# One graph transformer forward pass on one core: what the first gather of each edge beat waits for

## The chip, the cores and the metric

The kernel runs on one core of one Trainium2 chip. The metric is device time in microseconds (us); lower is better. TensorE is called PE below, VectorE DVE, ScalarE ACT, GpSimd POOL and SyncE SP, as the profile calls them.

## The reference, cut to what matters

The reference is a two-layer graph transformer on 625 nodes of width 1024 with 10,000 edges. The change lies in the first graph layer, an attention over edges (GATv2). Cut to its core, with H = 4 heads of 64:

```python
xl = (h @ Wl).reshape(n, H, D)            # h: the normed nodes, projected to 256
xr = (h @ Wr).reshape(n, H, D)
msg = xl[src] + xr[dst]                   # one row per edge
e = einsum('ehd,hd->eh', where(msg > 0, msg, 0.2 * msg), att)
alpha = softmax of e over the edges of each dst
out = segment_sum(alpha[..., None] * xl[src], dst) @ W_up
```

To this the reference adds a linear attention over the same nodes (q, k and v by 1024x1024 matrices, 16 heads). A quantised feed-forward block, a second graph layer, a second linear attention, an attention and a mixture of eight experts follow.

## The kernel before, in words

**The stages.** The kernel works in fp32 on tiles of 125 nodes (five of them, named by t). The edge stage of layer 0 stretches over the linear attention of layer 0, which gives PE its work while the edges are handled by the other engines. After it come the weighted sums over the edges, the feed-forward block, layer 1, and the experts, which take the second half of the time.

**The edge stage.** `xl` and `xr` lie in DRAM as `xl_d` and `xr_d`, 625 rows of 1 KB each. The edges are cut into 79 chunks of up to 128, and the chunks into 40 groups of two (the last group, number 39, has one chunk of 16 edges). A group goes through three steps:

- `gather(g, j, side)` (line 605, its DMA on line 611): an indirect DMA from POOL's queue fetches 128 rows of `xl_d` into tile `ga` (side 0) or of `xr_d` into `gb` (side 1). Each of `ga` and `gb` has five buffers, so that gather g overwrites what group g - 5 has used.
- `score_group(g)` (line 617; lines 621 and 591 to 594): four DVE operations make the edge scores `es`. ACT then raises them (`exp`, line 598).
- `scatter` (line 626, its DMA on line 631): an indirect DMA from POOL's queue writes 128 raised scores into the DRAM array `table`, one row of four per pair of nodes.

**The beats.** `one_beat()` (line 684) issues one step of this pipeline: on DVE the score of an earlier group, on ACT its exponential, and on POOL the four gathers of group g with scatters of earlier groups between them. `lags` says how far behind they run: the scores of group g - 4, the exponentials of g - 5 and the scatters of g - 6 belong to beat g; near the end (line 807) the lags become 1, 1 and 2. All engines execute in the order in which the program issues, which is written by hand: after each group of matmuls, `work(us)` (line 702) adds up an estimate of PE's time and issues a beat for every 8.6 us of it. In steady state a beat has six POOL instructions: ga, gb, table, ga, gb, table.

**The wait in question.** `group` (line 130) and the two other places that issue matmuls in this stage note the name of the last matmul in `latest["pe"]`. The first gather of each beat (`j == 0 and side == 0`) is made to wait for that matmul by `behind(got, latest["pe"])` (line 615). Since POOL's queue is in order, what stands behind this gather waits with it: the other gathers of the beat, and the scatters.

**The order around it.** PE runs the key and value projections (`pk`, `pv`), with counts of edges between them (`pct`), the states (`pkv`), the queries (`pq`), the answers (`pd`, `po`) and the output projection (`px`, line 745). DVE takes each result out of PSUM one step later than PE makes it (the class `Stream`), and a beat's score follows those. Between the keys and the queries the PSUM pool is exchanged, so the first `pq` needs the last `pv` to be read out. At the end the beats that are left are issued in a row (line 817). Then `load_table` (line 827) reads `table` back (tile `tb`), also from POOL's queue; DVE multiplies it with the counts (`pT`, line 841), and PE sums over it (`pg`).

Of the kernel before, what the change touches and what calls it, by code (L numbers as in the profile page):

```python
# [53 lines left out]
def attempt(ctx: ExitStack, tc: tile.TileContext, w: dict, out: bass.AP, shifted: bool):  # L54
# [78 lines left out]
    latest = {}  # L133

    def behind(ins, name):

        tc.add_manual_dep(ins.ins, name, mybir.DependencyInfo(mybir.DependencyClass.Sync,
                                                              mybir.DependencyReason.DATA), reason="pace")
        return ins
# [216 lines left out]
    with ExitStack() as st0:  # L356
# [8 lines left out]
        with ExitStack() as edges:  # L365
# [239 lines left out]
            def gather(g, j, side):  # L605
                lo, n, p = groups[g]
                if j == 0 and side == 0:
                    ab[g] = [pool.tile([128, G, 256], FP, tag=k, name=k, bufs=5) for k in ("ga", "gb")]
                if j < n:
                    src, ix = ((xl_d, si), (xr_d, di))[side]  # L610
                    got = nc.gpsimd.indirect_dma_start(  # L611
                        out=ab[g][side][0:p, j, :], out_offset=None, in_=src[:, :],
                        in_offset=bass.IndirectOffsetOnAxis(ap=ix[0:p, lo + j:lo + j + 1], axis=0))
                    if j == 0 and side == 0 and "pe" in latest:
                        behind(got, latest["pe"])

            def score_group(g):
                lo, n, p = groups[g]
# [65 lines left out]
            def one_beat():  # L684
                g = beat["g"]
                beat["g"] += 1
                if 5 <= g < NT + 5:
                    self_loops(g - 5)
                if lags[1] > lags[0]:
                    raise_all(g - lags[1])  # L690
                    scores(g - lags[0])
                else:
                    scores(g - lags[0])
                    raise_all(g - lags[1])
                for j in range(G):
                    if g < len(groups):
                        gather(g, j, 0)
                        scatter(g - lags[2] - 1)
                        gather(g, j, 1)
                    scatter(g - lags[2])  # L700
# [1271 lines left out]
```

## Time and profile before

| what | value |
|---|---|
| median of 3 runs | 2227.58 us (2226.61 to 2228.72) |
| the profiled execution, its own time | 2228.76 us |
| its span in the profile | 2227.0 us |
| mean granted PE clock | 0.977 |
| PE busy | 2112.5 us, 95% of the span |
| POOL busy | 341.4 us, 15% |
| first and last gather start | 57.6 and 423.4 us |
| first and last scatter start | 94.3 and 442.0 us |
| gathers on each side, scatters | 79, 79, 79; about 1 us of POOL each |

The profile is of one execution, which took 1.2 us more than the median. Its span is 1.8 us shorter than its own time. Times inside the profile are counted from the start of the span. A line of the timeline gives start, duration, engine, line, operation, and in brackets how long the engine had been idle and what ended that. For a DMA from POOL's queue the duration is that of POOL's instruction, and not of the transfer.

### The profile page before, as it was taken

What the parts mean: (1) busy time and instruction counts of PE and PEld (TensorE: products, weight loads), DVE (VectorE), ACT (ScalarE), POOL (GpSimd) and SP (SyncE); (2) the same over time, 40 slices, a digit from 0 to 9 for tenths busy, and PEclk for the clock granted to TensorE, in tenths of its full rate; (3) what the DMA queues carried; (4) which work ended last, traced back from release to release, by engine and by line L of the source; (5) the groups of instructions that cost most, each with busy time, mean ns of one, the idle gap of its engine ahead of it and who ended that gap; (6) DMA issues with size and microseconds to landing.
All of it is one profiled execution on the core that took longest, in us unless ns stands there. A gap on an engine that the chain in (4) does not pass through costs nothing. (4 is left out here: it accounts for less than half of the span.)

```text
span 2227.0 us, 17363 instructions
## 1 busy us (share of the span) xinstructions
PE 2112.5 (95%) x6934; PEld 1209.9 (54%) x6934; DVE 713.3 (32%) x1214; ACT 194.1 (9%) x354; POOL 341.4 (15%) x349
## 2 busy tenths in 40 slices
PE   8899799578899999999999999999999999999998
PEld 6466375245444777754445767557744444444443
DVE  5765467557623560000113133322011111111112
ACT  2000010001211100000000111100000000000000
POOL 1666656610000020210000000110000000000011
PEclk9999899878999999999999999999999999999999
DMA  9226252071122110231213111021099987997742
GB/s 299 77 62 209 59 182 81 25 212 33 38 85 71 52 38 1 85 142 38 76 38 104 38 38 38 20 103 61 34 347 337 331 325 282 327 331 286 275 144 92
DMA packets 145848, 301.62 MB, mean 135 GB/s; under 512 B 12370, under 2 KB 22436, under 8 KB 145754
## 3 DMA queue, kind: packets, MB, share of 16 engines
q1 hardware_dynamic: 123700, 244.23, 30.7%
q0 software_dynamic: 17376, 46.42, 7.1%
q10 hardware_dynamic: 4678, 9.72, 1.4%
q8 instruction: 58, 0.95, 0.2%
q14 instruction: 36, 0.29, 0.0%
HBM read 277.49 MB, written 22.84 MB: 135 GB/s over the span
## 5 line engine op out<-in xcount | busy, mean ns | idle before, releaser
L130 PE MATMUL pu<-w,xgT 128*128 128x512 f32 x768 | 333.9, 593 | 1.9 <-DVE xgT L1266 1.9
L130 PEld LDWEIGHTS pu<-w,xgT 128*128 128x128 f32 x768 | 144.0, 190 | 174.8 <-issue 171.7
L130 PE MATMUL pyb<-w,hb 128*128 128x512 f32 x384 | 174.3, 599 | 2.5 <-ACT yb L105 2.1
L130 PE MATMUL pq<-xnT,w 128*128 128x313 f32 x512 | 139.6, 432 | 13.8 <-DVE v L286 13.0
L130 PE MATMUL pk<-w,xnT 128*125 128x512 f32 x320 | 143.2, 599 | 3.3 <-issue 2.8
L130 PE MATMUL pv<-w,xnT 128*125 128x512 f32 x320 | 142.2, 597 | 1.5 <-issue 1.1
L130 PE MATMUL p<-tT,w 128*128 128x313 f32 x512 | 136.3, 428 | 0.4 <-DVE tT L1266 0.4
L130 PEld LDWEIGHTS pq<-xnT,w 128*128 128x128 f32 x512 | 98.2, 193 | 53.5 <-DVE v L286 13.8
L130 PEld LDWEIGHTS pyb<-w,hb 128*128 128x128 f32 x384 | 69.8, 189 | 90.9 <-issue 74.8
L1806 DVE TENSOR_TENSOR su<-pu,su 128x512 f32<-128x512 f32 x24 | 16.6, 692 | 314.6 <-ACT su L1805 314.6
L130 PEld LDWEIGHTS p<-tT,w 128*128 128x128 f32 x512 | 96.8, 190 | 37.9 <-issue 1.2
L130 PEld LDWEIGHTS pk<-w,xnT 128*125 128x125 f32 x320 | 59.8, 189 | 77.0 <-issue 76.1
L130 PEld LDWEIGHTS pv<-w,xnT 128*125 128x125 f32 x320 | 59.9, 189 | 75.4 <-issue 72.6
L1789 POOL DMA_INDIRECT xg<-rows_d,slots x12 | 11.4, 946 | 524.8 <-PE pxg L1796 449.0
L631 POOL DMA_INDIRECT table<-es,at x79 | 84.2, 1066 | 49.4 <-issue 26.2
L611 POOL DMA_INDIRECT ga<-xl_d,si x79 | 79.7, 1009 | 74.8 <-issue 33.2
L611 POOL DMA_INDIRECT gb<-xr_d,di x79 | 81.8, 1036 | 25.3 <-issue 22.8
L745 PE MATMUL px<-w,oT 128*125 128x512 f32 x160 | 69.8, 594 | 2.9 <-DVE x L909 2.0
L130 PE MATMUL px<-w,hT 128*125 128x512 f32 x160 | 70.3, 592 | 0.0
L130 PE MATMUL px<-w,oT 128*125 128x512 f32 x160 | 70.3, 592 | 0.0
L130 PE MATMUL ph<-meanT,w 128*128 128x313 f32 x256 | 70.1, 426 | 0.0
L130 PE MATMUL ph<-xnT,w 128*128 128x313 f32 x256 | 70.0, 427 | 0.0
(366 smaller groups left out, 2459.9 us busy)
## 6 DMA issues: line engine op xcount, KB each, us to landing
w<-in_eW_dram SPq DMA_DIRECT2D x144, 1024.0 KB
w<-in_L_Wk_dram SPq DMA_DIRECT2D x8, 1024.0 KB
w<-in_L_Wv_dram SPq DMA_DIRECT2D x8, 1024.0 KB
w<-in_L_Wq_dram SPq DMA_DIRECT2D x8, 1024.0 KB
w<-in_L_Wo_dram SPq DMA_DIRECT2D x8, 1024.0 KB
w<-in_W_self_dram SPq DMA_DIRECT2D x8, 1024.0 KB
w<-in_W_neigh_dram SPq DMA_DIRECT2D x8, 1024.0 KB
w<-in_sW_dram SPq DMA_DIRECT2D x8, 1024.0 KB
```

Source lines behind the costliest of these rows:

```text
L130: made = nc.tensor.matmul(dst, lhsT=lhsT, rhs=rhs, start=(i == 0), stop=(i == len(pairs) - 1))
L611: got = nc.gpsimd.indirect_dma_start(out=ab[g][side][0:p, j, :], out_offset=None, in_=src[:, :], in_offset=bass.IndirectOffsetOnAxis(ap=ix ...
L631: nc.gpsimd.indirect_dma_start(out=table[:, :], out_offset=bass.IndirectOffsetOnAxis(ap=at[0:p, lo + j:lo + j + 1], axis=0), in_=es[0:p, l ...
L745: made = nc.tensor.matmul(hold["px", t][:P, c, :], lhsT=oT[:, k, nodes(t)], rhs=wo[c](k), start=(k == 0), stop=(k == KC - 1 and keep is no ...
L1789: nc.gpsimd.indirect_dma_start(out=xg, out_offset=None, in_=rows_d[:, :], in_offset=bass.IndirectOffsetOnAxis(ap=slots[:, b:b + 1], axis=0))
L1806: nc.vector.tensor_tensor(su, pu[:, 0, :], su, op=ALU.mult)
```

## The change

The first gather of a beat no longer waits for the matmul noted last. It waits instead for the DMA of the gather issued last before it, which is the last `gb` of the beat ahead; waiting for a DMA means waiting until its data have landed. The first beat waits for neither. Nothing is moved: every engine issues the same instructions in the same order, and no other wait is taken away by hand. The buffers and the order of the writes to `table` still give waits of their own, as before.

```diff
                     got = nc.gpsimd.indirect_dma_start(
                         out=ab[g][side][0:p, j, :], out_offset=None, in_=src[:, :],
                         in_offset=bass.IndirectOffsetOnAxis(ap=ix[0:p, lo + j:lo + j + 1], axis=0))
-                    if j == 0 and side == 0 and "pe" in latest:
-                        behind(got, latest["pe"])
+                    if j == 0 and side == 0 and g:
+                        behind(got, latest["gather"])
+                    latest["gather"] = got.ins.name
```

Later lines of the changed kernel have numbers that are higher by one.

## The prediction

> **What bounds the kernel now.** I read the page first, for the stage.
>
> ```profile
> span 2227.0 us, 17363 instructions
> ...
> PE 2112.5 (95%) x6934; PEld 1209.9 (54%) x6934; DVE 713.3 (32%) x1214; ACT 194.1 (9%) x354; POOL 341.4 (15%) x349
> ...
> PE   8899799578899999999999999999999999999998
> ...
> POOL 1666656610000020210000000110000000000011
> PEclk9999899878999999999999999999999999999999
> ```
>
> PE is busy nearly everywhere; it dips only in the first ten slices of 55.7 us, and that is where POOL works. Whatever the change does, it does before about 460 us. Afterwards everything is relative to PE, so what is won or lost there reaches the end whole. Next, the table of windows over that stage (columns: window, its length, busy us of PE, PEld, DVE, ACT, POOL, granted clock, DMA share, GB/s).
>
> ```profile
> 260.00:280.00 20.00, 7.67 (x23) 5.40 (x24) 2.84 (x5) 0.00 (x0) 12.95 (x13) 0.66 0.20 59
> ...
> 420.00:440.00 20.00, 2.57 (x6) 0.77 (x5) 15.00 (x20) 0.41 (x2) 11.74 (x9) 0.64 0.02 3
> 440.00:460.00 20.00, 4.70 (x18) 3.95 (x18) 4.84 (x5) 0.00 (x0) 8.30 (x14) 0.50 0.71 162
> ```
>
> PE stands in two places. The second is the end of the edge stage; the timelines of POOL and of all engines give its chain.
>
> ```profile
> 375.38 0.99 POOL L631 DMA_INDIRECT table<-es,at  x1 [0.44 <-DMA table<-es,at]
> 384.86 0.96 POOL L611 DMA_INDIRECT ga<-xl_d,si  x1 [8.50 <-PE px L745]
> ...
> 396.72 1.48 POOL L611 DMA_INDIRECT ga<-xl_d,si  x1 [0.30 <-issue]
> 398.51 1.34 POOL L631 DMA_INDIRECT table<-es,at  x1 [0.30 <-issue]
> ```
>
> ```profile
> 442.03 0.85 POOL L631 DMA_INDIRECT table<-es,at  x1 [1.90 <-issue]
> 444.54 0.90 POOL L173 DMA_DIRECT2D tb<-table  x1 [1.66 <-issue]
> ...
> 453.14 4.84 DVE L841 TENSOR_TENSOR pT<-tb,CT 125x500 f32<-125x500 f32 x5 [16.54 <-DMA tb<-table]
> ...
> 454.23 0.68 PE L130 MATMUL pg<-xl,pT 125*125 125x65 f32 x2 [31.66 <-DVE pT L841]
> ```
>
> PE's last px ends at 422.6; it then waits 31.7 us for a chain that runs through POOL: last scatter, table read back, pT. From 384.86 on POOL has hardly a gap, and just before it stood 8.5 us for a matmul. That is the wait that the change removes.
>
> The first place is odd:
>
> ```profile
> 252.29 7.03 PE L130 MATMUL pv<-w,xnT 128*125 128x512 f32 x16
> 272.33 10.21 PE L130 MATMUL pq<-xnT,w 128*128 128x313 f32 x32 [13.01 <-DVE v L286]
> ```
>
> ```profile
> 271.59 0.69 DVE L286 TENSOR_TENSOR v<-pv,bv_t 125x512 f32<-125x512 f32 x1 [12.73 <-remote]
> ```
>
> The pv matmuls end at 259.3, but DVE, which needs only their semaphore, starts at 271.59, and POOL's next beat, which waits for PE too, at 271.82. PE's signal came 12 us late. It comes late elsewhere: kb at 80.67 for a pk ended at 73.8, kb at 157.77 for 153.2, v at 227.01 for 215.9. Each time the signal fell due late in a run of 21 to 40 us in which POOL had issued without a gap over 0.5 us (57.6 to 78.6, 131.7 to 155.4, 196.9 to 224.3, 228.8 to 268.6), and the signal came 2 to 3 us after POOL stopped. I take it, as an inference from four coincidences, that long unbroken runs of indirect DMAs delay PE's signals. The wait on PE then acts as a valve: late signals stop POOL.
>
> **What the Trainium skill says.** "Perfetto Trace Analysis", section "DMA Instruction — SWDGE (GPSIMD)": the shown end of such a DMA is that of making descriptors, and not of the data. The trace agrees: a gb takes 0.97 us of POOL, but the DVE operation waiting for it starts 2.92 us (406.84 to 409.76) and 3.00 us (417.83 to 420.83) after its start. "DMA: Bandwidth & Descriptors", section "Anatomy of one DMA — SWDGE (gpsimd) path", puts the fixed cost at about 2.0 us, mostly the write receipt; for 128 KB its formula gives an estimate of 2.3 us, consistent with 2.9 measured up to the waiter. I use the trace's 2.9. "TensorE: Matmul & The Clock Gate", Part 1: after an idle window PE runs at half clock until it has been busy some us. The trace agrees: 0.66 granted in 260 to 280, and the first pq took 10.2 us where later ones take 8.6. No page that I found speaks of PE's late signals.
>
> **The change, part by part.**
>
> *The new wait.* It covers landing, 2.9 us from the start of the last gb. In a steady beat one scatter stands between that gb and the next ga, so the next ga comes 2.56 us after it anyway (1.27 + 0.99 + 0.30). Cost: 0.35 us a beat; a beat grows from 7.64 (333.72 to 341.36) to 8.0 us. It is hidden by PE, which takes about 8.4 us of matmuls per beat; without that cover, 33 beats by 0.35 make 12 us, my upper bound. The first five or six beats have no scatter: there 1.27 becomes 2.9, a pause of 1.6 us, 6.7 us a beat for 5.1. Their scores are due only four beats later (score 2 ran at 89.1, its gathers would be in by about 80): no cost. Queued behind the waiting gather: the beat's gathers and scatters; waiting for these: scores, and at the end the table.
>
> *The old wait.* POOL now follows the landing and the buffers. Gather g needs score g - 5. Gather 25 started at 271.82 while score 20 was done at 249.4, so buffers would allow it 22 us earlier. Up to two beats of POOL's work are released that PE held back. DVE never waits for gathers except at the very end (16.6 us, three times), so earlier gathers by themselves bring nothing before that.
>
> *The end.* Counting back from the 16-edge group at 420.39, the ga at 384.86 is group 36 and the one at 396.72 group 37. Group 36 needs score 31 (done 364.3) and a landing at about 376.9: it starts at 377 and its beat, 11.9 us, ends by 389. What is late next is DVE: gather 37 overwrites group 32, whose score runs from 388.91 to 391.05, behind the weight sums (L767). So gather 37 starts at 391.3 for 396.72: 5.4 us won. Its first scatter needs the exponential at 391.27, met. Two more beats follow with 0.35 us each of new wait: 4.7 us. The gb at 401.36 stood 1.5 us behind POOL's queue; that may go or stay. I take **5 us**, with 4 and 7 as ends. Table, pT and pg follow; DVE, idle 16.5 us before pT, has room.
>
> *PE before 376 us.* From 45.0 on, PE lost against its own pace (10.87 us per group with six counts, 6.86 without): 5.5 us at 73 to 94, 8.7 by 113.5, 2.6 by 159.6, about 15 around 259 to 282, 5 later: some 37 us. This can go both ways. For: the early beats get pauses of 1.6 us more, which may save the 5.5; I take half, **2.7**. The middle I take as **0**: POOL's work is the same, and a DVE held up by a late signal still stops POOL through the buffers, only up to two beats later. Bounds: 18 us won if the 259 gap and the early slowness go, 30 us lost if the valve is missed.
>
> Sum: 5 + 2.7 = 7.7 us off the profiled 2228.8, or 2221.1; against the median, 1.2 lower, 2219.9. I say **2220**.
>
> **The rivals.** A measurement of this kernel can tell about 0.2%, 4.5 us, from no change.
>
> *Slower: the valve is gone.* Without PE's wait POOL runs unbroken as long as DVE's buffers allow. Where POOL lags behind DVE (97 to 165, 196 to 236, 300 to 345, the last two after weight loads have slowed it), signals get late after some 19 us and PE then goes at half speed (1.4 us from matmul to matmul at 99.6 to 104, normal 0.43). Two beats beyond cost PE 8 to 10 us a stretch. One stretch gives 10 - 5 = 5 us slower, 2233; three give 30 - 5 = 25, 2252. It decides once POOL's unbroken runs exceed those of before by more than about 10 us. Chance 0.39.
>
> *No change.* The early half and the middle cancel the end's gain, or DVE's place at 388.9 moves later by what PE loses: within 4.5 us of 2227.6. It also covers the case where the landing wait just replaces PE's in time, because both are met when DVE's is: 2227. Chance 0.17.
>
> *Faster by more.* POOL, bound to DVE beat by beat, gets a pause of half a us or more in each, and PE's signals stay on time: 13.0 + 1.6 + 5 + 5.5 off, about 2203. It shares the 0.44 for faster with the forecast.
>
> That the change doesn't do what it says can be left out: the program's order is unchanged, and one semaphore takes another's place.
>
> **How the numbers follow.** 0.44 faster, 0.17 same, 0.39 slower. The range goes from 2204 (end, early part and the 259 gap all won) to 2248 (most of three stretches lost); beyond these I leave 0.2. Within the faster case alone it would be 2205 to 2223.
>
> **What would show it.** Right: POOL no longer idle for 8 us before the gather of group 36, gather 37 just behind the score at 389 to 391, the last scatter 4 to 7 us after its place now relative to the last px, and PE's wait before pg at 25 to 28 us for 31.7. Early ga's 2.9 us behind the last gb. Wrong: pq's wait grown beyond 13 us, v or kb "remote" beyond 27.3 and 11.3 us in total, single slow matmuls in more places, or px ending after 425 us.

## The result, and the profile after

The changed kernel took 2232.40 us in the median of 20 runs (2226.69 to 2235.92), beside 2226.66 us (2223.11 to 2232.17) for the kernel before; the 20 runs of before hold the three of the table ahead of the prediction. The ratio is 1.0021, 95% interval [1.0013, 1.0029]: slower by 0.21%, 4.7 us, where the prediction said 7.6 us faster. The profiled execution after took 2226.69 us itself, the shortest of the changed kernel's runs; its span is 2224.9 us. The two profiled executions thus stand the other way round from the medians, the changed kernel's 2.1 us ahead, and the comparison below goes by stages and not by totals.

From the page of the changed kernel, the lines that answer to those shown of before:

```profile
span 2224.9 us, 17365 instructions
...
PE   7999999379899999999999999999999999999998
...
POOL 1575666610000010210000000110000000000011
PEclk9999999678999999999999999999999999999999
```

A slice is 55.6 us. The fifth slice of PE, 223 to 278 us, was at 7 tenths and is at 9 now; the eighth, 389 to 445, has gone from 5 to 3, and its granted clock from 8 to 6. The table of windows (window, length, busy us of PE, PEld, DVE, ACT and POOL with instructions, granted clock, DMA share, GB/s) says what became of the two places where PE stood:

```profile
260.00:280.00 20.00, 18.64 (x94) 14.59 (x93) 5.90 (x11) 4.11 (x10) 11.05 (x12) 1.00 0.54 188
420.00:440.00 20.00, 0.00 (x0) 0.00 (x0) 12.56 (x16) 0.25 (x2) 10.89 (x8) 0.50 0.01 1
440.00:460.00 20.00, 7.46 (x31) 6.71 (x31) 4.84 (x5) 0.00 (x0) 9.37 (x17) 0.50 0.82 204
```

The 7.67 us of PE at 260 to 280 have become 18.64: the late signal before the first pq is gone. At the end PE does nothing at all from 420 to 440. PE's timeline gives both waits:

```profile
254.87 8.70 PE L130 MATMUL pq<-xnT,w 128*128 128x313 f32 x32 [0.78 <-DVE v L286]
...
451.48 0.68 PE L130 MATMUL pg<-xl,pT 125*125 125x65 f32 x2 [38.86 <-DVE pT L842]
```

The first pq starts 17.5 us sooner than before (254.87 for 272.33), and PE's last px ends 10.0 us sooner (412.6 for 422.6). But pg starts only 2.8 us sooner (451.48 for 454.23): the chain that it needs has hardly moved, and PE waits 38.9 us for it instead of 31.7. And the timeline of POOL shows the new wait at work, early in the stage and in the middle:

```profile
58.05 0.95 POOL L611 DMA_INDIRECT gb<-xr_d,di  x1 [0.30 <-issue]
61.06 0.94 POOL L611 DMA_INDIRECT ga<-xl_d,si  x1 [2.06 <-DMA gb<-xr_d,di]
...
213.06 0.96 POOL L611 DMA_INDIRECT ga<-xl_d,si  x1 [1.30 <-DVE v L286]
...
218.13 0.95 POOL L611 DMA_INDIRECT gb<-xr_d,di  x1 [0.30 <-issue]
219.38 0.98 POOL L632 DMA_INDIRECT table<-es,at  x1 [0.30 <-issue]
221.56 0.96 POOL L611 DMA_INDIRECT ga<-xl_d,si  x1 [1.19 <-DVE CT L491]
```

The last `gb` of a beat starts at 218.13; the next beat's `ga` starts at 221.56, 3.43 us later, and 1.19 us after the scatter before it ended. The releaser named there (DVE's CT, or v at 213.06) is probably a coincidence: a pause of 1.2 to 1.3 us stands at the head of most beats from group 7 on, under several names, and it goes when the landing wait goes (below). A regular beat is 8.50 us (213.06 to 221.56). Before, it was 7.64 (333.72 to 341.36), and the scatter was followed by the next `ga` after the usual 0.30 us. From POOL's timeline of before:

```profile
333.72 0.97 POOL L611 DMA_INDIRECT ga<-xl_d,si  x1 [0.30 <-issue]
...
338.82 0.95 POOL L611 DMA_INDIRECT gb<-xr_d,di  x1 [0.30 <-issue]
340.07 0.99 POOL L631 DMA_INDIRECT table<-es,at  x1 [0.30 <-issue]
341.36 0.97 POOL L611 DMA_INDIRECT ga<-xl_d,si  x1 [0.30 <-issue]
```

**POOL's stage as a sum.** Since POOL's queue carries the beats, I take the starts of the first gathers of groups 0, 7, 36 and 39 in POOL's timeline, and pg in PE's. Every number is a difference of two start times. The first four rows are the two kernels in their first profiles and in later sets; all other rows, and those sets, follow below.

| kernel | group 0 starts | 0 to 7 | 7 to 36 (a beat) | 36 to 39 | 39 to pg | pg starts |
|---|---|---|---|---|---|---|
| before, first profile | 57.6 | 41.8 | 285.5 (9.84) | 35.5 | 33.8 | 454.2 |
| before, a later set (before_fourth) | 57.7 | 39.7 | 255.4 (8.81) | 35.5 | 33.4 | 421.8 |
| after, profile of the result | 54.2 | 51.7 | 276.0 (9.52) | 36.1 | 33.4 | 451.5 |
| after, a later set (after_again) | 58.1 | 51.1 | 276.4 (9.53) | 36.1 | 33.9 | 455.7 |
| no_wait | 55.2 | 39.6 | 253.8 (8.75) | 36.3 | 33.6 | 418.5 |
| pe_until_36 | 56.6 | 40.4 | 252.9 (8.72) | 35.3 | 33.4 | 418.7 |
| both_waits | 59.7 | 54.9 | 274.3 (9.46) | 36.2 | 33.9 | 459.1 |
| land_early | 57.1 | 49.6 | 255.4 (8.81) | 36.3 | 33.7 | 432.0 |
| land_late | 56.7 | 41.6 | 275.9 (9.51) | 36.1 | 33.9 | 444.1 |
| land_odd | 57.9 | 40.9 | 262.0 (9.04) | 36.4 | 33.8 | 431.2 |
| land_prev | 56.2 | 43.3 | 259.1 (8.94) | 35.7 | 33.5 | 427.9 |
| own_first | 57.6 | 53.6 | 277.2 (9.56) | 36.1 | 34.2 | 458.7 |

Two things stand out. Beside before_fourth, the landing wait costs POOL 10 to 15 us in groups 0 to 7 and 19 to 22 us from 7 to 36, in every kernel that has it there in every beat. From 7 to 36 land_odd and land_prev lose 7 and 4 us; where the wait is missing, the other rows but the first stay within 3 us of before_fourth. And the kernel before, in its first profile, lost 27 to 30 us between groups 7 and 36 that it lost in no later one (258.3 in before_again, 255.5 in before_third).

### The profile page after: what moved, and what is told of

It is laid out like the page before. It is cut to its first block, busy times and chain, and to the rows that moved or that the text cites. A ratio compares the mean times of both kernels' runs of the same rounds, so it can differ in the third digit from the quotient of the medians.

```text
span 2224.9 us, 17365 instructions
## 1 busy us (share of the span) xinstructions
PE 2112.3 (95%) x6934; PEld 1211.4 (54%) x6934; DVE 712.3 (32%) x1214; ACT 193.9 (9%) x354; POOL 338.9 (15%) x349
## 5 line engine op out<-in xcount | busy, mean ns | idle before, releaser
L1790 POOL DMA_INDIRECT xg<-rows_d,slots x12 | 11.3, 944 | 524.8 <-PE pxg L1797 449.0
L130 PE MATMUL pg<-xl,pT 125*125 125x65 f32 x200 | 32.0, 332 | 41.2 <-DVE pT L842 39.9
```

The source lines that it names most:

```text
L130: made = nc.tensor.matmul(dst, lhsT=lhsT, rhs=rhs, start=(i == 0), stop=(i == len(pairs) - 1))
L1790: nc.gpsimd.indirect_dma_start(out=xg, out_offset=None, in_=rows_d[:, :], in_offset=bass.IndirectOffsetOnAxis(ap=slots[:, b:b + 1], axis=0))
```

## The experiments

The theory after the result had two parts. (1) The landing wait lengthens POOL's beats, and POOL's chain, not PE's, sets the end of the edge stage; so the pauses are paid there. (2) What the change won beside that, the late signals of PE, belonged to the first set of runs and not to the kernel. The rivals: the prediction's valve (unbroken runs of POOL make PE's signals late), a cost of the wait instruction as such, and a loss that goes through ACT and PE early in the stage and not through POOL. Each kernel is compared with the kernel before on the same chip. Diffs are against the changed kernel unless said otherwise.

### Both kernels again, and neither and both waits

after_again is the changed kernel, unaltered. no_wait drops the three new lines, and with them every wait of this kind. both_waits keeps the new and restores the old:

```diff
+                    if j == 0 and side == 0 and "pe" in latest:
+                        behind(got, latest["pe"])
                     if j == 0 and side == 0 and g:
                         behind(got, latest["gather"])
```

pe_until_36 is the kernel before with its condition cut short:

```diff
-                    if j == 0 and side == 0 and "pe" in latest:
+                    if j == 0 and side == 0 and g < 36 and "pe" in latest:
```

The expectations of this first set rest on the first two profiles alone; the split above was not known yet.

> The changed kernel again, for a second profile and a ratio on the same chip as the other three. Its first profile was one of its fastest executions. Theory A (the landing wait makes POOL's own chain the bound): ratio to before 1.001 to 1.004, and whatever delays the first gather delays the end by the same, so first gather to last scatter is again about 386 us. Theory B (the loss of the wait on PE costs, the landing wait hardly): PE's late signals should be seen again, v and kb waiting over 10 us for matmuls that have ended.

> The first gather of a beat waits for neither a matmul nor a landing; buffers and table order alone hold it. Theory A: POOL's beat falls from 8.5 to about 7.6 us, so the last scatter comes earlier and the kernel is faster than the changed one by 5 us or more (2227 or less), and faster than before if PE's signals stay on time. Theory B: unbroken POOL runs make PE's signals late again, pq waits over 10 us for v, and the kernel is slower than the changed one, 2240 or more.

> The first gather waits for the matmul as before and for the landing as in the changed kernel. Theory A: the pauses keep PE's signals on time, so the wait on PE adds little to the changed kernel's time before the end; at the end the 8.5 us wait for px is back: 3 to 10 us slower than the changed kernel, 2236 to 2242. Theory B: the valve is back and the late signals are cured, so it is as fast as before or faster, 2227 or less.

> The kernel before, but from group 36 on the gathers wait for no matmul. It tests the step of the prediction that put 5 us (4 to 7) on the end alone: gather 36 at about 377 us, gather 37 just behind the score of group 32, ratio 0.998. If the end is not bound by that wait, ratio 1.000.

Measured, on a chip where the kernel before took 2197.94 us (27 runs):

| kernel | median us | ratio to before | 95% interval |
|---|---|---|---|
| after_again | 2231.34 | 1.0149 | [1.0132, 1.0165] |
| no_wait | 2197.31 | 0.9997 | [0.9988, 1.0007] |
| both_waits | 2234.69 | 1.0168 | [1.0155, 1.0181] |
| pe_until_36 | 2196.72 | 0.9991 | [0.9981, 1.0001] |

The changed kernel takes what it took before, 2231 us, but the kernel before is 29 us faster than in the set of the result. Here the price of the change is bare: 1.49%, 33 us. Without either wait there is no difference to before, so the old wait costs nothing here, and the landing wait costs all of it. Both waits together lie 3 us above the landing wait alone, but their intervals overlap.

The valve, in the form that long unbroken runs alone make PE's signals late, falls with no_wait. Its POOL runs from 55.22 to 97.02 us with no gap over 0.31 us, 42 us, and PE's signals come on time in it. From the timelines of DVE and PE of no_wait:

```profile
74.91 0.67 DVE L265 TENSOR_TENSOR kb<-pk,bk_t 125x512 f32<-125x512 f32 x1
```

```profile
241.67 8.70 PE L130 MATMUL pq<-xnT,w 128*128 128x313 f32 x32 [0.78 <-DVE v L286]
```

This kb belongs to a pk that ended at 73.9. In the first profile of before it stood until 80.67, in a POOL run that was only 21 us long. Long runs are thus not enough to delay PE's signals. The later profiles of before say the same: in before_fourth POOL runs without a gap over 0.5 us from 57.7 to 99.6 and from 215.8 to 265.1 us, longer than any run in the first profile, and no signal is late. What a kernel without the wait does in an execution that has late signals is not tested by this.

### The landing wait in a part of the beats

```diff
-                    if j == 0 and side == 0 and g:
+                    if j == 0 and side == 0 and 0 < g < 7:               # land_early
+                    if j == 0 and side == 0 and g >= 7:                  # land_late
+                    if j == 0 and side == 0 and g >= 7 and g % 2:        # land_odd
```

> The changed kernel with the landing wait in groups 1 to 6 only, where no scatter stands between the beats; the later beats wait for nothing. Theory A (two costs: the early pauses make ACT's writes of the diagonal late and with them the ring that PE waits for, 11 us and 3 us of half speed; the later pauses make POOL the bound at the end): +14 us, ratio 1.005 to 1.007, with PE waiting 8 to 11 us on ring at 106 to 125, and about 32 us before pg as without the waits. Rival B (only POOL's pace counts): within 3 us of no change, since POOL, 8.2 us a beat against PE's 8.4 or more, takes back its 10 us before the end. Rival C (the early part is all): +30 us.

> The changed kernel with the landing wait from group 7 on only; the early beats run unbroken. Theory A: PE waits under 4 us on ring; POOL's 32 beats are 0.65 to 0.9 us longer each, 21 to 29 us, of which the slack of POOL against PE hides some: +10 to +23 us, ratio 1.005 to 1.010; px waits on kept or oT, and the wait before pg is 36 to 41 us. Rival B (only POOL's pace counts): +21 to +23 us. Rival C (the early part is all): within 3 us of no change.

> The changed kernel with the landing wait in the odd groups from 7 on only, 17 of them where land_late had 33. Theory P (each pause of 0.9 us lengthens POOL's chain, less what the scatters behind it then wait less): half of the 20.8 us of land_late, +8 to +13 us, ratio 1.004 to 1.006. Rival (a single pause is taken up by the slack at the scatters, and only two in a row are paid): under +4 us.

Measured: land_early 2207.51 us, ratio 1.0034 [1.0023, 1.0045]; land_late 2221.44 us, 1.0094 [1.0074, 1.0114] (both beside 2198.39 us); land_odd 2206.47 us, 1.0039 [1.0027, 1.0051] (beside 2197.68 us on another chip). In us, as ratio less one times the median of before: 7.5, 20.7 and 8.6. The two parts sum to 28, against 33 for the whole; the intervals allow that they add up. Half of the pauses (17 of 33) cost 0.4 of land_late, 0.3 to 0.6 by the intervals. In the table a beat takes 9.51 us with all of them, 9.04 with every second and 8.7 to 8.9 with none. A pause of 0.9 us in 33 beats would be 29 us; part of it is given back at the scatters, whose idle time beyond 0.3 us sums to 22.8 us in land_late and to 34.4 in a later profile of before (before_third), because POOL comes to them later.

My expectation for land_early, 14 us, was too high. It came from PE, which I took to lose 14 us at 106 to 125 and to pass that on. The profile of land_early has 9.7 us of ring waits, and pg at 432.0, 10.3 us later than in before_fourth; POOL's groups 0 to 7 alone are 9.9 us longer there. So either account fits its size, and rival B, who lets POOL catch up, falls: POOL doesn't. own_first, below, tells the two accounts apart.

### Landing, or the wait as such

```diff
-                    latest["gather"] = got.ins.name
+                    if side == 0:
+                        latest["gather"] = got.ins.name
```

> The changed kernel with the wait put on the last but one gather of the beat ahead (its last ga, issued 1.27 us before the last gb) in every beat. If the landing is what costs (next ga no sooner than 3.4 us after the start of the gather waited for), then in a steady beat it is met at 3.4 - 1.27 = 2.1 us after the last gb, before POOL comes to it at 2.56: POOL's gap before ga is 0.3 us again, and the time is that without the waits plus what the early beats lose (0.5 us each): ratio 0.999 to 1.002. If the wait as such costs (a semaphore instruction on POOL's queue, met or not): the gap stays near 1.2 us and the ratio is 1.008 to 1.016.

Measured: 2205.60 us, ratio 1.0031 [1.0023, 1.0038]. From POOL's timeline, the same place in the beat as shown of after:

```profile
208.13 0.95 POOL L611 DMA_INDIRECT gb<-xr_d,di  x1 [0.30 <-issue]
209.38 1.05 POOL L633 DMA_INDIRECT table<-es,at  x1 [0.30 <-issue]
210.74 0.96 POOL L611 DMA_INDIRECT ga<-xl_d,si  x1 [0.30 <-issue]
```

A wait on a gather that was issued 1.27 us earlier leaves the gap at 0.30 us, and of some 33 us only 6.8 remain. What costs is thus to wait for a landing that comes after POOL is ready; a wait that is met by then costs nothing in this beat. The ratio lies above what I expected (0.999 to 1.002). About 3 us of it are the pauses of the early beats, 0.5 us each as expected (43.3 from group 0 to 7 for 39.7); for the rest the profile shows one pause of 2.67 us at 220.83 behind DVE's v, and I have no cause for the remainder.

### Does the loss go through ACT and PE?

Both kernels have another coupling that the prediction missed. In beats 5 to 9 ACT's queue writes the diagonal of `table` (`self_loops`, line 173), in order with the scatters' landing. With POOL late these writes are late, ACT stands behind them, DVE behind ACT, and PE behind DVE's `ring`. ACT's longest such wait was 9.0 to 10.1 us in the three later profiles of before; in the changed kernel it is 16.3. From the timelines of ACT and PE of the changed kernel:

```profile
106.77 0.21 ACT L598 ACTIVATE es<-es 128x8 f32<-128x8 f32 x1 [16.31 <-DMA table<-es,at]
```

```profile
110.56 2.88 PE L467 MATMUL pct<-ring 128*125 128x313 bf16 x10 [2.99 <-DVE ring L446]
118.55 4.18 PE L467 MATMUL pct<-ring 128*125 128x313 bf16 x15 [5.11 <-DVE ring L446]
```

At 100 to 120 us this leaves PE 11.90 us busy of 20, its largest loss before the px. own_first takes it away by putting the self loops ahead of the first scatter; before_own_first does the same to the kernel before:

```diff
-                if 5 <= g < NT + 5:
-                    self_loops(g - 5)
+                if g < NT:
+                    self_loops(g)
```

> The changed kernel with the five node tiles' self loops in beats 0 to 4 instead of 5 to 9, so that ACT's writes of the diagonal are issued before the first scatter and have no scatter's landing to wait for. Theory P (POOL sets the end from its first gather to its last scatter, and its landing pauses are untouched): PE's waits on ring fall from 8 to 11 us to under 3, ACT's 16 us stand before an es goes, and the time stays: against the kernel before the ratio is 1.012 to 1.018, as for the changed kernel. Theory E (PE's loss at 106 to 125 us passes to the end): 8 to 11 us of the 33 go: ratio 1.009 to 1.012.

> The kernel before with the self loops in beats 0 to 4. Where PE's signals are on time its POOL chain held 3.3 us in which a scatter waited for ACT's write of the diagonal, and PE stood 5.3 us on ring. Theory P: POOL's 3 us go and nothing else: -1 to -4 us, ratio 0.998 to 0.9995. Theory E: PE's 5 us go too: -5 to -9 us, ratio 0.996 to 0.998. Rival (the self loops' DVE work in the first beats holds up the ring instead): +2 us or more.

Measured: own_first 2232.14 us, ratio 1.0149 [1.0129, 1.0170], the same as the changed kernel; before_own_first 2197.98 us, 1.0002 [0.9992, 1.0012]. PE's waits in own_first, from the table of waits (who waited, for whom, us in total, times, longest):

```profile
PE pg L130 <- DVE pT L842: 39.5, 5, 38.4
PE pq L130 <- DVE v L286: 15.7, 1, 15.7
PE px L746 <- DVE kept L753: 7.6, 1, 7.6
PE pct L467 <- DVE ring L446: 3.0, 1, 3.0
```

This is the clearest line of the study. PE's wait on ring fell from 8.1 (11.3 in after_again) to 3.0 us, and more than that came back at the first pq, 15.7 us for 0.8: v stands on DVE behind a score, and the score waits for `gb`. From DVE's timeline of own_first:

```profile
256.37 0.69 DVE L622 TENSOR_TENSOR ga<-ga,gb 128x512 f32<-128x512 f32 x1 [5.54 <-DMA gb<-xr_d,di]
...
259.25 0.68 DVE L286 TENSOR_TENSOR v<-pv,bv_t 125x512 f32<-125x512 f32 x1
```

The pv ended at 244.3. PE got ahead and met POOL later. The time did not move, so the loss passes through POOL, and the ring was only the place where PE happened to wait for it. In before_own_first, the 1 to 4 us that I expected from POOL's wait for the diagonal didn't show; the longest such wait was 3.6 us in the profile that I read it from (before_again), and 1.7 and 1.8 us in two others.

### The kernel before, in later sets

before_again, before_third and before_fourth are the kernel before, unaltered; after_third and no_wait_again are the changed kernel and no_wait, in one set with before_fourth. One run of each.

> The kernel before, unchanged, for a profile of it on the chip of these runs. Theory A (PE's late signals belonged to the chip or execution of the first profile, not to long runs of indirect DMAs): v follows its pv at once, PE waits under 1.5 us at the first pq, PE waits nowhere else between 45 and 385 us, as in the kernel without either wait; one time within 0.3% of the other runs of the kernel before. Rival (the late signals are the kernel's own): a wait of 8 us or more at the first pq, and kb or v idle for PE's signal 3 to 12 us in one or more places.

> The kernel before again, for a profile of it on whatever chip this set runs on. Where the runs of before give about 2198 us: PE's signals on time, under 1.5 us before the first pq, extra idle of POOL before its first gathers of a beat under 3 us in all. Where they give about 2227 us: PE's signals late as in the first profile, a wait of 8 us or more at the first pq, and 30 us or more of POOL idle before first gathers.

> The kernel before once more, on whatever chip this set runs on. If it gives about 2227 us as in the first profile: PE's signals late, a wait of 8 us or more at the first pq, over 25 us of POOL idle before first gathers of a beat. If about 2198 us: none of these.

> The kernel with neither wait, on the same chip. Where the kernel before gives about 2227 us there: if the late signals cost through the wait on PE, no wait gives about 2198 us; if unbroken runs of POOL make the signals late (the prediction's rival), it is as slow or slower, 2227 to 2252 us, with v and kb late by 30 us or more in all. Where the kernel before gives about 2198 us: 2195 to 2201 us.

> The changed kernel, on the same chip: 2226 to 2236 us on either kind of chip, with the first pq waiting under 1.5 us and POOL's landing pauses 41 us or more in all; if late signals reach this kernel too, v waits over 5 us for PE's signal and the time is over 2240 us.

Measured: before_again 2203.45 us, before_third 2196.96, before_fourth 2197.70; no_wait_again 2199.53, after_third 2233.13. The first of these misses its bounds in one place, 5.3 us of PE on ring; none has a late signal. From before_fourth's timelines of PE and DVE, at the place that was odd in the first profile:

```profile
238.40 7.03 PE L130 MATMUL pv<-w,xnT 128*125 128x512 f32 x16
246.22 8.69 PE L130 MATMUL pq<-xnT,w 128*128 128x313 f32 x32 [0.79 <-DVE v L286]
```

```profile
245.47 0.69 DVE L286 TENSOR_TENSOR v<-pv,bv_t 125x512 f32<-125x512 f32 x1 [3.33 <-PE pv L130]
```

The pv ends at 245.4, v starts at 245.47: no delay, where the first profile had 12 us. The instructions are the same, 17363 of them. In the first profile not only signals were late: between 45 and 420 us PE itself stood 13.5 us, in 21 pauses of up to 1.1 us, with nothing that the profile shows to wait for, and no later profile of before, of no_wait or of the changed kernel has such a pause. Where the prediction saw PE at half speed, at 99.6 to 104 us, the granted clock is 1.00, and its matmuls stand 0.8 us apart. So the kernel before took 2223 to 2232 us in each of the 20 runs of the result's set, and 2197 to 2203 us (medians and single runs) in four later sets on four different chips, while the changed kernel took 2231 to 2233 us in each set that had it. What slowed before in the first set was therefore not an accident of one execution. On which chip that set ran is not on record, so the chip remains one possible cause. It did not come back, and the cause is open. Whether no_wait would have been fast in the first set too was not tried for that reason. That the changed kernel shows no late signal in the result's profile is observed; that its pauses are what prevents them is a guess.

No version here beats the kernel before: no_wait, pe_until_36 and before_own_first are the same as it.

## Why the prediction was wrong, point by point

**What bounds the kernel: the step that failed.** The new wait was to be "hidden by PE, which takes about 8.4 us of matmuls per beat". It was not, because PE does not bound this stage. The line for it was in the prediction: PE waits 31.7 us before pg, for a chain that runs through POOL. That wait is slack of PE against POOL's whole chain, back to the first gather, and I read it as a matter of the last beats. In no_wait PE waits under 2 us in all from 45 us to the end of its last px, at 386, and then 32.5 us for pg; in own_first, time that PE gains is lost again at the next place where it meets POOL. With POOL as the bound, the working for the early and middle beats turns over: "hidden by PE" becomes paid, less what POOL then waits less at its scatters.

**The size of the new wait.** 0.35 us a beat was forecast, from the 2.9 us at which a waiting DVE had started, less POOL's 2.56. Measured: 3.43 us in a beat with a scatter, so 0.87, 2.5 times the forecast. In the early beats, without a scatter, 61.06 is 3.0 us behind the start of the gb ahead of it (58.05), as forecast. Uncovered, 33 such pauses would be 29 us; land_late gives 20.7, since part comes back at the scatters. The upper bound of 12 us was too low.

**"No cost" for the early pauses.** The pauses were sized rightly, 6.9 us a beat (54.20 to 61.06) for 6.7, but they cost 7.5 us (land_early), and through the diagonal's writes they reach ACT, DVE and PE within 50 us. The cover named, that scores come four beats later, concerned DVE and not POOL.

**The old wait: "earlier gathers by themselves bring nothing".** Right in the later sets (no_wait, 0.9997): POOL's idle time beyond 0.3 us before its `ga` was 0.7 to 3.1 us in all in the three later profiles of before. In the first profile it was 41.1 us, and 30 us of POOL's chain from group 7 to 36 went with it. There the change had something to win, and the changed kernel's 49.8 us of such idle time took its place.

**The end, 5 us.** One predicted sign is there, POOL's idle time of 8.5 us before group 36 is gone:

```profile
373.04 0.96 POOL L611 DMA_INDIRECT ga<-xl_d,si  x1 [1.21 <-DMA gb<-xr_d,di]
...
381.96 0.96 POOL L611 DMA_INDIRECT ga<-xl_d,si  x1 [1.21 <-DMA table<-es,at]
```

These are groups 35 and 36, 8.9 us apart, where before had 16.0. But group 36 starts only 2.9 us sooner than before (381.96 for 384.86, forecast 377), since the pauses of the beats ahead had made group 35 4.1 us later (373.04 for 368.91). And where signals are on time, removing just that wait is worth 2 us, 4 at most (pe_until_36, 0.9991 [0.9981, 1.0001]); and PE's wait before pg grew to 38.9 us instead of falling to 25 to 28. From group 36 on nothing was won: 36.1 us to group 39 for 35.5.

**PE before 376.** The upper bound, 18 us won "if the 259 gap and the early slowness go", is nearest to what happened at the first pq: 17.5 us sooner. The choice of 0 for the middle was wrong on both sides: the late signals went, and the pauses took their place. The two nearly cancelled on POOL's chain, 41.77 + 285.45 before and 51.74 + 276.02 after; that is 327.2 and 327.8 us. The rival "no change" has the words for it, "the landing wait just replaces PE's in time", at 2227, and was given 0.17; its reason, that both are met when DVE's wait is, is not what happened. That 2232 lies as near to 2220 as it does, inside the range of 2204 to 2248, is luck: a loss of some 30 us, taken as hidden, met a gain of nearly the same size, of which 2.7 us had been counted.

**The valve.** The rival "slower: the valve is gone" has the right sign by a wrong mechanism: no signal was late after the change, and neither of these marks ("remote" beyond 27.3 and 11.3, a longer wait at pq) appeared. Four coincidences in one execution were too few to rest a mechanism on.

**The skill's figures.** From "DMA: Bandwidth & Descriptors", "Anatomy of one DMA — SWDGE (gpsimd) path", the prediction estimated 2.3 us for such a DMA, and took 2.9 from the trace. In after_again the gathers' landing is 2.8 us from issue in the median (2.2 at least), and the next DMA of POOL starts 3.0 to 3.4 us from the start of the one it waits for: the formula's estimate is near the shortest landing, and not what the queue loses. The same section says that a wait is taken on the issuing sequencer, ahead of the dispatch; the trace agrees, the pause stands on POOL's queue with all six instructions of the beat behind it.

## What to carry to other kernels

An engine that waits long at the end of a stage may have had slack in all of it, as PE had here: look for the chain it waits for, add up that chain's starts from the first link on, and price the change there. A wait for a DMA's landing, in the queue that issues the next one, cost here the time from issue to landing and restart less what already stood between, and part of that came back at later waits of the same queue; waiting for the transfer one earlier made it free in the steady beats. And one profile can hold delays that don't come back in later sets; before a mechanism is built on them, see whether a later set on another chip has them.

## What the runs showed of the hardware that I had not expected

- One program, the kernel before, took 2227 us in one set and 2197 to 2203 us in four others, with PE's signal for v 12 us late in the first profile and within 0.1 us in that of before_fourth. The changed kernel's medians and single runs in three sets lie within 2 us (2231.34 to 2233.13).
- On POOL's queue the next DMA started 3.43 us after the start of the awaited one with a scatter between, and 3.0 us without. A wait already met left the usual gap of 0.30 us. What the 0.4 us between the two are was not taken apart.
